# Two mixtures of experts in one network kernel: finished rows out of the first, other memory and PSUM pools at the start of the second

## The chip, the cores and the metric

The kernel runs on one core of a Trainium2 chip. The metric is the device time of one execution in microseconds. Each kernel is run several times, and the median stands for it. A profile of one further execution shows every instruction of the five engines: TensorE (PE, its weight loads PEld), VectorE (DVE), ScalarE (ACT), GpSimd (POOL), and SyncE (SP), which here only issues DMA transfers.

## The reference

The reference is a network of four layers on a graph of 2708 nodes with 256 features in fp32. Each layer adds a graph part and a feed-forward part to `x`, both on a layer norm of `x`:

```python
x = x + gnn(layernorm(x), adj, ...)      # L0 cosine attention, L1 GAT of 4 heads, L2 and L3 GAT of one head
x = x + ffn(layernorm(x), ...)           # L0 slices, L1 first mixture, L2 decoder with second mixture, L3 linear
```

The change touches the two mixtures. The first (layer 1) sends every node to one of eight experts:

```python
H = gelu(xf @ W1 + b1)                                   # 2708 x 1024, common to all experts
probs = softmax(H @ Wg + bg)
assign = argmax(probs)
out = sum over e: where(assign == e, probs[:, e] * (H @ Wd[e] + bd[e]), 0)
```

The second is the feed-forward half of a decoder block (layer 2). Causal attention of four heads comes first, and then every node goes to its two best of eight experts:

```python
x = x + attention(rmsnorm(x, ln1)) @ wo.T
flat = rmsnorm(x, ln2)
tp, ti = top_k(softmax(flat @ router_w.T), 2); tp = tp / sum(tp)
out = sum over e: weights[:, e] * ((silu(flat @ w1[e].T) * (flat @ w3[e].T)) @ w2[e].T)   # HID 682
```

## The kernel before, in words

`X` holds the node features in on-chip memory (SBUF) as 22 row tiles of 128 nodes, the last of 20. All parts of the network read it and add into it. The program is written with tiles and pools: a tile waits for whatever last used its memory, and where a pool is opened over memory of a pool that has been closed, the first writer of each new tile waits for the last user of the old one. Within an engine the order is the scheduler's, and `issue_after` pins an instruction behind another one.

**First mixture** (`top1_ffn`, 980 to 1258 us of the span). Blocks of four row tiles are taken through W1 and gelu. `store` turns the 1024 hidden values of each node back to rows and writes them from SP to `hidden`, a table in DRAM with one row per node. The router's `logits` are made on the way, and `Routing.chunk` places each node in a slot of its expert and scatters the node numbers into `fnodes` from POOL. When all of it has landed, `numbers` reads the list back, and a loop (`through`, 26 slot tiles) goes over tiles of 128 slots which belong to one expert each: `fetch` gathers 128 rows of `hidden` by an indirect DMA into one of five `hr` buffers, `transposes` turns them on TensorE into `ht`, sixteen matmuls with `wd` give `y`, DVE adds the bias into `ys`, and `Routing.send` scatters the rows to `fys`, a table in DRAM in the order of the nodes. `route.weights` computes the chosen probability of every node once (softmax8) while the first rows are fetched. `combine` then loads `fys` into tiles `y0` and sums `X += weight * y` by a DVE instruction per row tile.

**GAT g2** (`gat_single`) starts as soon as the first four tiles of `X` are summed: layer norm statistics, `f`, transposes `tp`, projections `pv`, and then the long loop of `acc` products (L1483). g3, after the second mixture, is the same function. For the second mixture `combine` has another branch: `X` itself lies in the table `dys` from before (`keep` writes it there), the experts' results are added to it by the scatter, and nine SP loads bring finished rows back into `X`.

**Attention and the second mixture** (`attention`, `experts`; 1516 to 2298 us). Attention goes over six column groups of up to 512 nodes. After the last key tile of a group, `close` sums the denominators `pd` on TensorE and DVE divides (`reciprocal`, multiply into `yt`, or `yl` for the last group). `send` of a group then takes it through `wo` (`wy`), adds a normalised X (`xa`), forms the row `h` for the experts, its router logits and the slots, and scatters `h` from POOL into `hs`, the experts' table in DRAM. These sends run spread over the next group's attention. The last group's send runs beside the first expert tiles, and the eight scatters of the last but one group come at the very end of attention. The rows of the first eight slot tiles are loaded into X's tiles (free by then, since the rows are kept in `dys`) ahead of that, and two of them are transposed there.

`experts` takes slot tiles through `h` = w1 (half 0, then SiLU) and w3 (half 1, then the gate), transposes `pt`, and w2 (`po`). The w3 weights (`w<-in_d_w3T`) are loaded by SP at the handover. Its PSUM pools and its SBUF pools `e_work` and `e_r` lie over those of attention: `ss`, `xa`, SiLU's `warm` tile and `hh` are their first tiles. Both halves of `h` lie in one pool `e_h` of four banks, of which one was attention's.

Of the kernel before, what the change touches and what calls it, by code (L numbers as in the profile page):

```python
# [35 lines left out]
def rows(t):  # L36
    return min(P, N - t * P)
# [957 lines left out]
def softmax8(nc, pool, p, n, r, name):  # L995

    m = pool.tile([P, n], F32, name=f"{name}x")
    b = m[:r].unsqueeze(2).to_broadcast([r, n, 8])
    nc.vector.tensor_reduce(m[:r], p, AX.X, ALU.max)
    nc.vector.tensor_tensor(p, p, b, ALU.subtract)  # L1000
    nc.scalar.activation(p, p, AF.Exp)
    nc.vector.tensor_reduce(m[:r], p, AX.X, ALU.add)
    nc.vector.reciprocal(m[:r], m[:r])
    nc.vector.tensor_tensor(p, p, b, ALU.mult)


def top1_ffn(net, ctx):
# [7 lines left out]
    with ExitStack() as inner:  # L1015
# [19 lines left out]
        rows_of = dram.tile([N, HID], F32, name="hidden")  # L1035

        with tc.tile_pool(name="f1tp", bufs=2, space=PSUM) as ptp, tc.tile_pool(
# [57 lines left out]
            def gate(its, halves, nw):  # L1095
                ht = [half[:, k, :] for half in halves for k in range(KC // 2)]
                pq = pg.tile([P, 512], F32, name="pq")
                for c in range(KC):
                    g = c % 4 * 32
                    nc.tensor.matmul(pq[g : g + 32, :nw], wg[:, c, :], ht[c][:, :nw], start=c < 4, stop=c >= 4)  # L1100
                q4 = rp.tile([P, 512], F32, name="q4", tag="hr", bufs=3)
                nc.vector.tensor_copy(q4[:, :nw], pq[:, :nw])
                pr = pg.tile([P, 4, E], F32, name="pr")
                for k, t in enumerate(its):
                    r = rows(t)
                    nc.tensor.matmul(pr[:r, k, :], q4[:, k * P : k * P + r], add4, start=True, stop=True)
                    nc.vector.tensor_tensor(route.logits[:r, t, :], pr[:r, k, :], bg[:r], ALU.add)
                for _ in route.chunk(rp, pg, its[0], len(its), None):
                    pass
# [13 lines left out]
            for n, (n0, nw) in enumerate(blocks):  # L1123
                its = tiles_of(n0, nw)
                halves = hidden(ft, nw)
                if n + 1 < len(blocks):
                    ft = features(tiles_of(*blocks[n + 1]))
                if n == 0:
                    for m in range(3, len(blocks)):
                        turn(add, m, ptp, "tp")  # L1130
                        turn(stats.sums, *tiles[m], root=False)
                    turn(stats.newton, rp, tiles[3][0], NT)
                    last = None
                    held.close()
                    wd = inner.enter_context(tc.tile_pool(name="f1wd", bufs=1, side="right"))
                    wd = wd.tile([P, E, KC, D], F32, name="wd")
                gate(its, halves, nw)
                kept.append((its, halves))
                if n + 2 < len(blocks):

                    stored = store(*kept.pop())
                    with tc.issue_after(stored.ins):
                        for e in range(2 * n, 2 * n + 2):
                            nc.sync.dma_start(wd[:, e], a["f1_wd"][e].rearrange("(c p) m -> p c m", p=P))
# [9 lines left out]
        with tc.tile_pool(name="f1t", bufs=1, space=PSUM) as pt, tc.tile_pool(  # L1154
# [34 lines left out]
            def fetch(s):  # L1189
                hr = held[s] = sp.tile([P, 2, 4, P], F32, name="hr", bufs=5)  # L1190
                return nc.gpsimd.indirect_dma_start(
                    out=hr.rearrange("p n c m -> p (n c m)"),
                    out_offset=None,
                    in_=rows_of[:, :],
                    in_offset=bass.IndirectOffsetOnAxis(ap=number[:, s : s + 1], axis=0),
                )

            def transposes(s):
                hr = held.pop(s)
                ht = sp.tile([P, 2, 4, P], F32, name="ht")  # L1200
                for n in range(2):
                    ps = pt.tile([P, 4, P], F32, name=f"ht{n}", bufs=2)
                    for c in range(KC // 2):
                        nc.tensor.transpose(ps[:, c, :], hr[:, n, c, :], net.ident)
                    (nc.scalar.copy if n else nc.vector.tensor_copy)(ht[:, n], ps)
                return ht

# [19 lines left out]
            route.weights(one)  # L1227
            heads = []

            def through(s0, s1, ready):  # L1230
                last = added = folding = None
                for s in range(s0, s1):
                    with tc.issue_after(last.ins) if last else nullcontext():
                        e = expert(nc.tensor, s)
                    this = ready
                    if s + 1 < s1:
                        ready = transposes(s + 1)
# [8 lines left out]
                    added = nc.vector.tensor_tensor(y, ps, bd[:, e, :].rearrange("p e d -> p (e d)"), ALU.add)  # L1246
# [325 lines left out]
class Routing:  # L1572
# [10 lines left out]
    def __init__(self, net, pool, dram, choices, key):  # L1583
# [12 lines left out]
        self.weight = pool.tile([P, choices, NT], F32, name=f"{key}weight")  # L1596
# [56 lines left out]
    def chunk(self, work, psum, t0, n, source, tag="pr"):  # L1653
# [42 lines left out]
        to = work.tile([P, self.choices, n], I32, name=f"{key}to")  # L1696
# [153 lines left out]
    def weights(self, work):  # L1850

        nc, E = self.net.nc, self.E
        p = work.tile([P, NT, E], F32, name=f"{self.key}p")
        nc.vector.tensor_copy(p, self.logits)
        softmax8(nc, work, p, NT, P, f"{self.key}sm")
        for c in range(self.choices):
            pc = work.tile([P, NT, E], F32, name=f"{self.key}pc")
            nc.vector.tensor_tensor(pc, p, self.one[:, c], ALU.mult)
            nc.vector.tensor_reduce(self.weight[:, c, :], pc, AX.X, ALU.add)

# [48 lines left out]
    def combine(self, pool):  # L1909

        net, nc, X = self.net, self.net.nc, self.net.X
        loaded = []
        queues = nc.sync, nc.gpsimd
        if self.choices == 2:
            for t0, t1 in ((0, 1), (1, 2), (2, 4), (4, 8), (8, 12), (12, 16), (16, 20), (20, NT)):
                for k0, k1, r in whole_and_rest(range(t0, t1)):
                    r0 = (t0 + k0) * P
                    self.read = nc.sync.dma_start(
                        X[:r, t0 + k0 : t0 + k1, :],
                        self.ys[r0 : r0 + (k1 - k0 - 1) * P + r, :].rearrange("(t p) d -> p t d", p=r),  # L1920
                    )
            yield
            return
        for n, (n0, nw) in enumerate(chunks(512)):
            its = tiles_of(n0, nw)
            ys = []
            for c in range(self.choices):
                y = pool.tile([P, 4, D], F32, name=f"y{c}", bufs=len(chunks(512)))
                for k0, k1, r in whole_and_rest(its):
                    r0 = (c * NT + its[k0]) * P  # L1930

                    engine = nc.scalar if n == 0 and c else queues[(n + c) % 2]
                    read = engine.dma_start(
                        y[:r, k0:k1, :],
                        self.ys[r0 : r0 + (k1 - k0 - 1) * P + r, :].rearrange("(t p) d -> p t d", p=r),
                    )
                    if engine is nc.gpsimd:
                        self.read = read
                ys.append(y)
            loaded.append((its, ys))  # L1940
        for its, ys in loaded:
            for k, t in enumerate(its):
                r = rows(t)
                for c, y in enumerate(ys):
                    last = nc.vector.scalar_tensor_tensor(
                        X[:r, t, :], y[:r, k, :], self.weight[:r, c, t : t + 1], X[:r, t, :], ALU.mult, ALU.add
                    )
            yield last


def attention(net, route, ln2, router, weights, mixture):
# [11 lines left out]
    with ExitStack() as ctx:  # L1963
# [98 lines left out]
        outs, sums, es = {}, {}, {}  # L2062
# [48 lines left out]
        def close(n, p):  # L2111
# [8 lines left out]
            for i in range(0, iw, half):  # L2120
                y = results[n][:, p : p + m, i : i + half]
                nc.vector.reciprocal(y, by_pairs(pd, m, iw)[:, :, i : i + half])  # L2122
                nc.vector.tensor_tensor(y, y, by_pairs(po, m, iw)[:, :, i : i + half], ALU.mult)

        def send(n, rp, aux, tag="aux"):
# [4 lines left out]
            nc.vector.memset(ss, 1.0)  # L2130
            xs, hs = {}, {}
            for k, t in enumerate(its):
# [4 lines left out]
                net.normed(xa, t, ln)  # L2137
                nc.vector.tensor_tensor(xa[:r], po[:r], xa[:r], ALU.add)
                nc.gpsimd.tensor_tensor(X[:r, t, :], X[:r, t, :], xa[:r], ALU.add)
                h = hs[t] = rp.tile([P, D + 4], F32, name="h", bufs=len(its) + 1)  # L2140
# [128 lines left out]
def experts(net, route, weights, head, first, fts, after, rest):  # L2269
# [7 lines left out]
    with ExitStack() as ctx:  # L2277
        work = ctx.enter_context(tc.tile_pool(name="e_work", bufs=2))
        pf = ctx.enter_context(tc.tile_pool(name="e_f", bufs=1, space=PSUM))
        ph = ctx.enter_context(tc.tile_pool(name="e_h", bufs=1, space=PSUM))  # L2280
        py = ctx.enter_context(tc.tile_pool(name="e_y", bufs=1, space=PSUM))
# [25 lines left out]
        def hidden(s, n, q):  # L2307
            if q == 0:
                halves[s, n] = ph.tile([P, 2, 512], F32, name=f"h{n}")
# [30 lines left out]
        def results(s, ht):  # L2340
            po = py.tile([P, D], F32, name="po")
            for k in range(KC):
                last = nc.tensor.matmul(  # L2343
                    po, ht[:KP, k, :], w2[:KP, es[s], k, :], start=k == 0, stop=k == KC - 1
# [3 lines left out]
            nc.scalar.activation(y, po, AF.Copy, scale=share)  # L2348
# [98 lines left out]
def biased_gnn(net, head, route):  # L2447
    def results(ctx):
        return route.combine(ctx.enter_context(net.tc.tile_pool(name="g2y", bufs=1)))
# [4 lines left out]
def elu_gnn(net, kept, head, route, tail):  # L2454
    def results(ctx):
        rest = route.combine(ctx.enter_context(net.tc.tile_pool(name="g3y", bufs=1)))
# [219 lines left out]
```

## Time and profile before

| | us |
|---|---|
| median of 3 runs | 2573.68 (2572.01 to 2580.48) |
| profiled execution | 2582.8 |
| its span, first to last instruction | 2580.9 |
| TensorE busy in it | 2420.4 |
| mean granted TensorE clock | 0.967 |

In the lines of the profile that follow, a row of the timeline gives the start, the duration, the engine, the source line, the operation, what it writes and reads, and in brackets the idle time of the engine before it with what ended that. A row of the chain of waits gives a start, a duration and who held the chain. "x8" is the number of instructions that are drawn together.

### The profile page before, as it was taken

To read this page: it belongs to the slowest core of one execution; us is meant where nothing else is said; L and a number is where in the kernel's file an instruction comes from. 1 tells how busy PE (TensorE), PEld (TensorE's weight loads), DVE (VectorE), ACT (ScalarE), POOL (GpSimd) and SP (SyncE) were. 2 spreads that over 40 slices of the span, in tenths; PEclk is the share of its full clock that TensorE was granted. 3 is DMA by queue.
4 is the path that set the end of the run, shared out by engine and by line. 5 is a ranking of instruction groups with operands and counts; after the bars stand their busy time and mean duration, and the time that the engine had idled before them with its cause. 6 is when DMAs were issued, how large, how long until landed. Compare 5 with 4: busy or idle time off the path is not lost.

```text
span 2580.9 us, 32654 instructions
## 1 busy us (share of the span) xinstructions
PE 2420.4 (94%) x11708; PEld 1575.2 (61%) x11708; DVE 1473.2 (57%) x3362; ACT 1049.6 (41%) x1687; POOL 357.0 (14%) x465
## 2 busy tenths in 40 slices
PE   5899998999999999979799989999979999979999
PEld 4666765686333334558678864444457777757887
DVE  7753437745888886433544457878853222243566
ACT  3444443213877782321344333434422222234444
POOL 1000003100000001134230011222222211210011
PEclk9999999969999999989899999999989999989999
DMA  8899512000000002665230010101332222140001
GB/s 287 291 290 345 186 47 73 1 6 1 1 1 1 1 1 84 161 175 168 78 94 1 1 33 17 36 18 50 112 112 49 34 34 34 27 146 29 1 1 44
DMA packets 113657, 197.98 MB, mean 77 GB/s; under 512 B 8898, under 2 KB 72768, under 8 KB 110658
## 3 DMA queue, kind: packets, MB, share of 16 engines
q1 hardware_dynamic: 92008, 150.88, 18.3%
q0 software_dynamic: 18496, 40.89, 6.3%
q10 hardware_dynamic: 2990, 4.06, 0.5%
q8 instruction: 98, 1.61, 0.3%
q14 instruction: 65, 0.53, 0.1%
HBM read 132.97 MB, written 62.83 MB: 76 GB/s over the span
## 4 chain that ended last, share of the span: by engine, by line
PE 42%; DVE 5%; DMA 3%; ACT 1%; issue 1%; POOL 0%; SPq 0%; DVEq 0%; POOLq 0%; ACTq 0%
PE acc L1483 14%; PE h L2311 8%; PE po L2343 4%; PE sc L2078 3%; PE po L2103 3%; PE pv L143 2%; PE pj L2049 2%; DMA dys<-y,to 2%; DVE sum L2109 2%; PE pt L2335 1%; DVE yt L2122 1%; PE acc L143 1%; PE s1p L1378 1%; PE wy L143 1%; DVE e L736 1%
## 5 line engine op out<-in xcount | busy, mean ns | idle before, releaser
L736 DVE SCALAR_TENSOR_TENSOR e<-e,mask 128x768 f32<-128x768 f32 (+3 forms) x352 | 418.1, 1218 | 222.2 <-ACT e L735 218.8
L735 ACT ACTIVATE e<-big_p,minus_one,ratio 128x768 f32<-128x768 f32 (+3 forms) x352 | 418.8, 1226 | 278.2 <-PE acc L1483 189.9
L1483 PE MATMUL acc<-V,e 128*128 128x257 f32 x1848 | 404.3, 381 | 5.7 <-DVE e L736 5.5
L1483 PEld LDWEIGHTS acc<-V,e 128*128 128x128 f32 x1848 | 351.3, 190 | 58.5 <-issue 6.5
L2311 PE MATMUL h<-w,ft 128*128 (+1 forms) x720 | 222.1, 450 | 0.0
L311 PE MATMUL acc<-F,e 128*128 128x257 f32 (+1 forms) x924 | 212.5, 383 | 3.8 <-DVE e L307 3.5
L932 PE MATMUL acc<-e,V 128*64 128x512 f32 (+1 forms) x1056 | 209.6, 549 | 1.3 <-DVE e L736 1.3
L311 PEld LDWEIGHTS acc<-F,e 128*128 128x128 f32 (+1 forms) x924 | 171.6, 189 | 56.6 <-DVE e L307 29.3
L2328 DVE TENSOR_TENSOR hh<-hh,h 128x682 f32<-128x682 f32 x47 | 40.7, 866 | 240.5 <-PE h L2311 240.5
L932 PEld LDWEIGHTS acc<-e,V 128*64 128x64 f32 x1056 | 73.8, 138 | 151.5 <-issue 145.9
L2311 PEld LDWEIGHTS h<-w,ft 128*128 128x128 f32 x720 | 129.1, 189 | 52.2
L307 DVE TENSOR_TENSOR e<-e,mask 128x512 f32<-128x512 f32 (+2 forms) x132 | 80.4, 620 | 140.8 <-ACT e L300 139.1
L2087 ACT ACTIVATE e<-sc 128x1024 f32<-128x1024 f32 (+4 forms) x131 | 107.2, 862 | 113.5 <-PE sc L2078 89.1
L2109 DVE TENSOR_TENSOR sum<-sum,e 128x1024 f32<-128x1024 f32 (+4 forms) x131 | 136.7, 1043 | 20.3 <-PE po L2103 11.2
L300 ACT ACTIVATE e<-score 128x512 f32<-128x512 f32 (+2 forms) x132 | 69.4, 544 | 170.7 <-PE score L298 145.3
L2343 PE MATMUL po<-w,ht 114*128 (+1 forms) x564 | 129.7, 379 | 0.9 <-DVE ht L2336 0.9
L2078 PE MATMUL sc<-qt,kt 64*128 64x512 f32 (+5 forms) x568 | 120.5, 542 | 1.4 <-ACT sum L2087 0.9
L2343 PEld LDWEIGHTS po<-w,ht 114*128 114x128 f32 x564 | 106.5, 189 | 22.6 <-DVE ht L2336 8.2
L943 PE MATMUL den<-e,low 128*3 128x512 f32 (+1 forms) x1056 | 117.7, 542 | 0.0
L298 PE MATMUL score<-QK 128*128 128x512 f32 (+2 forms) x264 | 112.1, 553 | 3.4 <-ACT e L300 3.0
L2103 PE MATMUL po<-e,V 128*64 128x512 f32 (+5 forms) x524 | 106.9, 525 | 1.9 <-DVE e L2093 1.9
L1895 POOL DMA_INDIRECT dys<-y,to x47 | 73.6, 1567 | 202.6 <-ACT ft L2293 184.5
(652 smaller groups left out, 3378.0 us busy)
## 6 DMA issues: line engine op xcount, KB each, us to landing
row<-in_adj SPq DMA_DIRECT2D x21, 1354.0 KB
raw<-in_adjT SPq DMA_DIRECT2D x35, 768.0 KB
hs<-zero SPq DMA_DIRECT2D x8, 2860.0 KB
hidden<-hr SPq DMA_DIRECT2D x32, 256.0 KB
wd<-in_f_wd SPq DMA_DIRECT2D x8, 1024.0 KB
kept<-mask SPq DMA_DIRECT2D x21, 338.5 KB
mask<-kept SPq DMA_DIRECT2D x21, 338.5 KB
w<-in_d_w1T SPq DMA_DIRECT2D x8, 682.0 KB
```

Source lines behind the costliest of these rows:

```text
L298: nc.tensor.matmul(ps[:r, :iw], QK[:, 0, span(j)], QK[:, 1, i0 : i0 + iw], start=True, stop=True)
L311: ended = nc.tensor.matmul(acc[k], e[:r, k * P : (k + 1) * P], F[:r, j, :], start=j == 0, stop=j == NT - 1)
L735: nc.scalar.activation(v, big_p[:, i], AF.Relu, bias=net.minus_one, scale=ratio)
L736: return nc.vector.scalar_tensor_tensor(v, v, 1.0, net.mask[:, j, i], ALU.add, ALU.mult)
L932: nc.tensor.matmul(acc[n][half, :iw], V[:, j, h, :], e[n][:, k, :iw], start=j == 0, stop=j == NT - 1)
L943: nc.tensor.matmul(den[g : g + Q, :iw], low[:, j, h, Q - 1 - q : 2 * Q - 1 - q], e[n][:, k, :iw], start=False, stop=j == NT - 1 and q == Q ...
L1483: nc.tensor.matmul(acc[k][:ri], e[:, k * P : k * P + ri], V[:, j, :], start=j == 0, stop=j == NT - 1)
L2078: nc.tensor.matmul(by_pairs(ps[:r, g], m, iw)[:, :, o:], kt[b, span(j)], qt[b, :, o:iw], start=True, stop=True)
L2103: nc.tensor.matmul(by_pairs(outs[n, p][b], m, iw)[:, :, o:], V[:r, j, g, :], by_pairs(e[:r, g], m, iw)[:, :, o:], start=j == 0, stop=j == ...
L2109: nc.vector.tensor_tensor(total, total, by_heads(e[:r], m, iw)[:, :, :, o:], ALU.add)
L2311: last = nc.tensor.matmul(halves[s, n][:, q, :HALF], fts[s][:, c, :], weights.w13[n][:, es[s], c, q * HALF : (q + 1) * HALF], start=c == 0 ...
L2343: last = nc.tensor.matmul(po, ht[:KP, k, :], w2[:KP, es[s], k, :], start=k == 0, stop=k == KC - 1)
```

## The change

In the first mixture the rows of `hidden` become longer: 1024 hidden values, the node's eight logits and its 256 values of `X`. `keep_rows` writes the two additions from POOL. The fetched row then holds all that is needed for the finished result: `share` computes the probability of the chosen expert from the logits per slot tile (maximum, subtraction, exp with a sum on ACT, reciprocal), and one more DVE instruction forms `ys * share + X`. `softmax8`, `Routing.weights` and the first branch of `combine` go. `fys` now holds finished rows, and both mixtures load them into `X` by the same nine SP transfers. `ht` has two buffers rather than three.

In the second mixture, the `h` rows of the last but one send are put into tiles of `X` that are free then (from tile 11 on) rather than into the pools which the experts take over. The slots `to` get two buffers in the routing's own pool. The experts' PSUM is opened as separate pools, in the order `e_f`, `e_h0` (half 0), `e_y` (`po`), `e_h1` (half 1) and `e_t` (`pt`), so that half 0 no longer shares a bank with attention's `po`. And in `send`, the memset of `ss` and the normalised `xa` are pinned behind the multiply that ended the last `close`.

```diff
-        rows_of = dram.tile([N, HID], F32, name="hidden")
+        rows_of = dram.tile([N, HID + E + D], F32, name="hidden")
+
+        def keep_rows(its, at, src):
+            for k0, k1, r in whole_and_rest(its):
+                r0 = its[k0] * P
+                nc.gpsimd.dma_start(
+                    rows_of[r0 : r0 + (k1 - k0 - 1) * P + r, at : at + src.shape[2]].rearrange("(t p) d -> p t d", p=r),
+                    src[:r, its[k0] : its[k0] + k1 - k0, :],
+                )
...
+                keep_rows(its, HID, route.logits)
...
                 kept.append((its, halves))
+                keep_rows(its, HID + E, X)
...
-                hr = held[s] = sp.tile([P, 2, 4, P], F32, name="hr", bufs=5)
+                hr = held[s] = sp.tile([P, HID + E + D], F32, name="hr", bufs=5)
...
-                hr = held.pop(s)
-                ht = sp.tile([P, 2, 4, P], F32, name="ht")
+                hr = held[s][:, :HID].rearrange("p (n c m) -> p n c m", n=2, c=4)
+                ht = sp.tile([P, 2, 4, P], F32, name="ht", bufs=2)
...
+            def share(s):
+
+                logits = held[s][:, HID : HID + E]
+                top, w = (sp.tile([P, 1], F32, name=n) for n in ("top", "share"))
+                nc.vector.tensor_reduce(top, logits, AX.X, ALU.max)
+                nc.vector.tensor_scalar(logits, logits, top, None, ALU.subtract)
+                nc.scalar.activation(logits, logits, AF.Exp, accum_out=w)
+                nc.vector.reciprocal(w, w)
+                return w
...
-            route.weights(one)
...
+                    with tc.issue_after(added.ins) if added else nullcontext():
+                        w = share(s)
                     if s + 1 < s1:
                         ready = transposes(s + 1)
...
-                    added = nc.vector.tensor_tensor(y, ps, bd[:, e, :].rearrange("p e d -> p (e d)"), ALU.add)
+                    nc.vector.tensor_tensor(y, ps, bd[:, e, :].rearrange("p e d -> p (e d)"), ALU.add)
+                    added = nc.vector.scalar_tensor_tensor(y, y, w, held.pop(s)[:, HID + E :], ALU.mult, ALU.add)
...
-        to = work.tile([P, self.choices, n], I32, name=f"{key}to")
+        to = self.pool.tile([P, self.choices, 4], I32, name=f"{key}to", bufs=2)[:, :, :n]
...
+    def combine(self):
+
+        for t0, t1 in ((0, 1), (1, 2), (2, 4), (4, 8), (8, 12), (12, 16), (16, 20), (20, NT)):
+            for k0, k1, r in whole_and_rest(range(t0, t1)):
+                r0 = (t0 + k0) * P
+                self.read = self.net.nc.sync.dma_start(
+                    self.net.X[:r, t0 + k0 : t0 + k1, :],
+                    self.ys[r0 : r0 + (k1 - k0 - 1) * P + r, :].rearrange("(t p) d -> p t d", p=r),
+                )
+        yield
...
-                nc.vector.tensor_tensor(y, y, by_pairs(po, m, iw)[:, :, i : i + half], ALU.mult)
+                ended[:] = [nc.vector.tensor_tensor(y, y, by_pairs(po, m, iw)[:, :, i : i + half], ALU.mult)]
...
-            nc.vector.memset(ss, 1.0)
+            with tc.issue_after(ended[0].ins):
+                nc.vector.memset(ss, 1.0)
...
-                net.normed(xa, t, ln)
+                with tc.issue_after(ended[0].ins):
+                    net.normed(xa, t, ln)
...
-                h = hs[t] = rp.tile([P, D + 4], F32, name="h", bufs=len(its) + 1)
+                if n + 2 == len(cols):
+                    h = done[:, 11 * D + k * (D + 4) : 11 * D + (k + 1) * (D + 4)]
+                else:
+                    h = rp.tile([P, D + 4], F32, name="h", bufs=len(its) + 1)
+                hs[t] = h
...
-        ph = ctx.enter_context(tc.tile_pool(name="e_h", bufs=1, space=PSUM))
-        py = ctx.enter_context(tc.tile_pool(name="e_y", bufs=1, space=PSUM))
+        ph = [ctx.enter_context(tc.tile_pool(name="e_h0", bufs=1, space=PSUM))]
+        po = ctx.enter_context(tc.tile_pool(name="e_y", bufs=1, space=PSUM))
+        ph.append(ctx.enter_context(tc.tile_pool(name="e_h1", bufs=1, space=PSUM)))
+        py = ctx.enter_context(tc.tile_pool(name="e_t", bufs=1, space=PSUM))
```

More of the change, by code (lines that the diff above doesn't have):

```diff
@@ L992, in first_max @@
     return oh, mx
[L995 to L1004, printed above, removed]
 def top1_ffn(net, ctx):
@@ L1189, in fetch @@
             def fetch(s):
-                hr = held[s] = sp.tile([P, 2, 4, P], F32, name="hr", bufs=5)
+                hr = held[s] = sp.tile([P, HID + E + D], F32, name="hr", bufs=5)
                 return nc.gpsimd.indirect_dma_start(
-                    out=hr.rearrange("p n c m -> p (n c m)"),
+                    out=hr,
                     out_offset=None,
@@ L1595, in __init__ @@
         self.one = pool.tile([P, choices, NT, E], F32, name=f"{key}one")
-        self.weight = pool.tile([P, choices, NT], F32, name=f"{key}weight")
         self.tag = pool.tile([P, NT, 4], F32, name=f"{key}tag")
@@ L1848, in others @@
             yield
[L1850 to L1859, printed above, removed]
     def load(self, s, f):
@@ L1907, in send @@
         return i
[L1909 to L1948, printed above, removed]
+    def combine(self):
[7 more added lines that the diff above has]
+        yield
 def attention(net, route, ln2, router, weights, mixture):
@@ L2060, in by_heads @@
             return t[..., : m * iw].rearrange("p g (m i) -> p g m i", m=m)
-        outs, sums, es = {}, {}, {}
+        outs, sums, es, ended = {}, {}, {}, []
         def scores(n, p, j):
@@ L2308, in hidden @@
             if q == 0:
-                halves[s, n] = ph.tile([P, 2, 512], F32, name=f"h{n}")
+                halves[s, n] = ph[n].tile([P, 2, 512], F32, name=f"h{n}")
             for c in range(2):
@@ L2340, in results @@
         def results(s, ht):
-            po = py.tile([P, D], F32, name="po")
+            ps = po.tile([P, D], F32, name="po")
             for k in range(KC):
                 last = nc.tensor.matmul(
-                    po, ht[:KP, k, :], w2[:KP, es[s], k, :], start=k == 0, stop=k == KC - 1
+                    ps, ht[:KP, k, :], w2[:KP, es[s], k, :], start=k == 0, stop=k == KC - 1
                 )
@@ L2347, in results @@
             to, share = tos.pop(s)
-            nc.scalar.activation(y, po, AF.Copy, scale=share)
+            nc.scalar.activation(y, ps, AF.Copy, scale=share)
             route.send(to, y)
@@ L2448, in results @@
     def results(ctx):
-        return route.combine(ctx.enter_context(net.tc.tile_pool(name="g2y", bufs=1)))
+        return route.combine()
     gat_single(net, "g2", head, results)
@@ L2455, in results @@
     def results(ctx):
-        rest = route.combine(ctx.enter_context(net.tc.tile_pool(name="g3y", bufs=1)))
+        rest = route.combine()
         first = next(rest)
```

## The prediction

> **What bounds the kernel now.** I read the page's busy table first, then the chain of waits, then the timeline at the chain's steps that are not TensorE, and last the DMA view there.
>
> ```profile
> PE 2420.4 (94%) x11708; PEld 1575.2 (61%) x11708; DVE 1473.2 (57%) x3362; ACT 1049.6 (41%) x1687; POOL 357.0 (14%) x465
> ...
> 1258.80 6.63 DMA y<-fys
> 1269.60 3.53 PE pv L143 x8
> ...
> 1889.68 5.90 DMA hs<-h,dto
> 1896.46 1.92 DVE yl L2122
> 1898.93 4.92 PE h L2311 x8
> ```
>
> TensorE is busy 94% of the span, and the change removes next to no matmul. So only TensorE's idle time, 160 us in all, can be won. The chain shows two idle places that the diff touches: the end of the first mixture (from 1257.8) and the handover from attention to the second mixture (from 1886). The timeline has both:
>
> ```profile
> 1255.36 0.96 POOL L1895 DMA_INDIRECT fys<-ys,to  x1 [2.49 <-DVEq L1847]
> 1257.92 1.51 SPq L1933 DMA_DIRECT2D y<-fys  x3
> 1261.75 1.67 DVE L1945 SCALAR_TENSOR_TENSOR X<-y,fweight,X 128x256 f32<-128x256 f32 x4 [3.07 <-DMA y<-fys]
> 1269.53 3.59 PE L143 MATMUL pv<-g2w,ft 128*128 128x257 f32 x8
> ...
> 1885.46 0.72 PE L2117 MATMUL pd<-sum,ones 128*64 128x296 f32 x4 [0.29 <-ACT X L2255]
> 1886.27 6.79 SPq L1568 DMA_DIRECT2D w<-in_d_w3T  x8
> 1889.68 0.96 POOL L1707 DMA_INDIRECT hs<-h,dto  x1 [0.30 <-issue]
> 1895.73 0.06 DVE L2130 MEMSET ss<- 128x4 f32 x1 [11.09 <-DMA hs<-h,dto]
> 1896.39 1.99 DVE L2122 RECIPROCAL yl<-pd 128x296 f32<-128x296 f32 x1
> 1898.93 4.92 PE L2311 MATMUL h<-w,X 128*128 128x341 f32 x8 [12.75 <-DVE yl L2123]
> 1903.64 1.33 PE L143 MATMUL wy<-wo,yl 128*128 128x256 f32 x4
> 1904.81 2.46 PE L2311 MATMUL h<-w,X 128*128 128x341 f32 x8
> ```
>
> At the handover DVE stands at the memset of ss until the last scatter of hs has landed, and the reciprocal queued behind it needs only pd, finished at 1886.18. TensorE's first expert product (h, half 0) waits 12.75 us for that DVE chain, since its PSUM tile shares a bank with attention's po. It then runs at half clock: 4.92 us for eight, against 2.46 us for the eight of half 1. From there on TensorE is full until 2291.
>
> **The change, part by part.** *1. Handover.* The h rows of the last but one send move out of the pools which the experts take over, the slots `to` too, and half 0 has its own banks. In the changed order DVE runs reciprocal and multiply of yl before ss and xa, and h half 0 waits for no DVE instruction. Step by step from 1886.18: h half 0 at 1886.3 to 1888.8 (2.46 us, the clock being full until then); yl done at 1886.3 + 1.99 + 0.1 + 0.46 = 1888.9; wy 1.04 us to 1890. Next is h half 1, which needs the first w3 expert. Its eight DMAs of 682 KB are issued from 1886.27 as before, beside the scatters. What moved, in the table by stretches (start:end, length, busy times, clock, DMA share, GB/s):
>
> ```profile
> 1886.00:1888.00 2.00, 0.18 (x2) 0.00 (x0) 0.00 (x0) 0.00 (x0) 1.70 (x2) 1.00 0.58 102
> 1888.00:1890.00 2.00, 0.00 (x0) 0.00 (x0) 0.00 (x0) 0.00 (x0) 1.39 (x3) 1.00 0.88 295
> 1890.00:1892.00 2.00, 0.00 (x0) 0.00 (x0) 0.00 (x0) 0.00 (x0) 0.65 (x1) 0.65 1.01 338
> ```
>
> By 1891 that is 0.20 + 0.59 + 0.34 = 1.13 MB, of which up to 0.5 MB are scatters; 0.68 MB of w3 fit. If the queue serves its transfers in order, expert 0 has landed at 1890.8 to 1891.5, and half 1 starts at 1891.4 instead of 1904.81: **-13.4 us**. The Trainium skill speaks against the order ("DMA: Bandwidth & Descriptors", section "Queues, rings and completion order"): completion is not FIFO per issuing engine, and an engine takes packets from its queues in turn. With all eight transfers sharing alike, expert 0 would end near 1904 and only -0.5 us would be left. The nearest row decides: of nine loads issued together on SP at 2297.98 the first (128 KB) let DVE start 1.97 us later, far ahead of the rest.
>
> ```profile
> 2297.98 5.22 SPq L1918 DMA_DIRECT2D X<-dys  x9
> 2299.95 0.43 DVE L164 BATCH_NORM_STATS2 bnst<-X 128x6 f32<-128x256 f32 x1 [6.45 <-DMA X<-dys]
> ```
>
> I take -13.3; ends -0.5 and -14. The eight scatters stay POOL's; the hh memset ahead of them waits for the same cast that they wait for. SiLU's table load (1.28 us) goes ahead of ACT's copies of X: ACT idles 2.24 us there, so 0; without that gap, +1.3. Later weights come every 1.7 us (682 KB at 400 GB/s), where a tile takes 8.16 us, and the first eight tiles' rows were loaded at 1794 to 1798.
>
> *2. End of the first mixture.* Rows come out finished, so the y tiles and 22 DVE sums go (0.42 to 0.48 us each, 10 us); nine SP loads write X itself, starting with one tile. From fys landed (1257.77) to the first loop product (1312.22) are 54.45 us. GAT g3 has just that form after the second mixture: landed 2297.91, loop 2347.24, 49.33 us. **-5.1**; -8 if all the sums lay on the path, -4 if they hide more. The w2 loads, which waited for the y tiles, start up to 28 us earlier, behind X's loads on SP: 0.
>
> *3. First mixture's loop.* A tile takes TensorE 4.33 us (26 tiles). DVE had 0.42 + 0.69; the share adds a reduce, subtract, reciprocal (0.17 each), a wait for ACT's exp (0.4) and the final sum (0.48). In sequence with gaps some 3.3 to 3.9 us, under 4.33: **0**; the last tile's sum lies bare: **+0.5**. A fetched row grows from 4096 to 5152 bytes, and its buffer (five) is freed by the sum rather than by the transposes:
>
> ```profile
> L1191 POOL DMA_INDIRECT hr<-hidden,number x26: 933/962/1021, 1134.7 to 1227.2; - x26
> ...
> DMA to landing us min/median/max: 4.1/4.8/8.5
> ```
>
> After sum s come the send (1.28 us of POOL with its gap), then fetch s+5, whose rows are wanted when y of s+3 ends, 3 x 4.33 - 1.0 us after sum s: a lead of about 10 us. 1.26 times the bytes make 4.8 us 6.0: 0. The first fetches, which nothing covers (5.07 us idle for the first, 0.45 for the second), get longer: **+0.7**. The removed weights (2.3 us of DVE, exp) lay beside this wait: 0.
>
> *4. Its preparation.* X (seven DMAs, 2.77 MB) and the logits (seven, 2708 pieces of 32 bytes) go out on POOL's queue ahead of and between the fnodes scatters, each of which they delay by at most two issues (1.3 us each). X is final by 1018.4; only 0.15 of the DMA time is used in 1000 to 1020 and the first scatters wait until 1024.78, so at 255 GB/s about 9 of 11 us of writes fit before the rest disturbs; TensorE's lead covers most. In 1115 to 1130 the DMA is full and bounds the first fetch. There the page's section "Specifications" warns: below 512 B a transfer misses line rate, by a read-modify-write. The fnodes pieces (4 bytes) are the row: 192 of them took 1.3% of 16 engines over 17 us, 0.018 us each. The last two groups of logits, 660 pieces, are then 660 x 0.018 / 16 = 0.75 us of the full stage; priced double for the rule, 1.5. I take **+1** for the stage (0 to +3.5; +14.6 if all of X, at 190 GB/s, displaced the stores).
>
> *5. Attention.* DVE is 9.67 of 12 us busy before the first projection (TensorE idles 6.08 us at 1516.44 to 1522.52). ss and two pairs of xa leave there: 0.49 + 0.53 + 0.40 + 0.40 + 0.06 = **-1.9**. They come back behind a multiply later, where TensorE has 19 to 20 of 20 us busy and DVE slack: 0 (-1 to +2).
>
> Sum: -13.3 - 5.1 + 0.5 + 0.7 + 1 - 1.9 = **-18**. The profiled execution took 2582.8 us (span 2580.9) and would become 2565; the median of the runs is 2573.7, 9 us less, so I subtract from that: **2556 us**.
>
> **The rivals.** *(a) The w3 weights become the bound.* The wait moves from yl to the first w3 expert at 1904. For it: 5.6 MB at 400 GB/s end just then. Against: the row of nine loads. Sum: -18 + 12.8 = -5, 2568. *(b) Slower: the fetch lead.* At the loop of the first mixture each fetch depends on the sum five tiles back. The cycle spans four tiles, so beyond a landing of L = 10 us every tile costs (L - 10)/4, over 26 tiles 6.5 us per us of L. L = 12.8 eats the gain, L = 14 makes +8 us, 2582. For it: a landing of 8.5 us occurs already, times 1.26 is 10.7. Against: the median is 4.8 and the DMA is 0.45 busy in 1150 to 1250. *(c) DVE or ACT turns becomes the loop's pace:* the share's hops through ACT take 0.4 us a tile more than TensorE's 4.33: +10, so -8, 2566. *(d) The change does nothing:* pools or queues still hold the wait in another form (a bank, a queued memset), -5 to 0, 2571.
>
> **How the numbers follow.** About 0.3%, 7.7 us, is what a measurement of this kernel tells from no change. The forecast has 0.68 (own range 2548 to 2565), (a) 0.10, (b) 0.09, (c) 0.08, (d) 0.05. Faster by over 7.7 us: 0.66 of the forecast, half of (c), a little of (a): 0.72. Slower: (b) and a full collision of X's writes together with (a): 0.10. Within: 0.18. The range 2547 to 2571 takes in (a), (c) and most of (d).
>
> **What would show it.** After: DVE's recip yl straight after pd, before ss; h half 0 starts within 1 us of pd, at 2.46 us for eight; half 1 waits 1 to 2 us for w3 (12 us: rival a). From fys landed to g2's loop 49 to 50 us. The loop at 4.33 us a tile, PE waiting for hr only at its start (each later wait: rival b; for ht: c). From the first hidden store to the first transposes at most 2 us longer. The forecast is wrong if h half 0 still names DVE, or if the front keeps its 54 us.

## The result, and the profile after

The changed kernel takes 2563.63 us (median of 16 runs, 2557.04 to 2572.08), the kernel before 2580.36 us in the same series (16 runs). The ratio of the two is 0.9943, with a 95% interval of 0.9930 to 0.9956. That is a gain of 14.7 us, between 11.4 and 18.1 (the medians lie 16.7 us apart, the means 14.7). The prediction said 2556 us, 18 us less than the three runs then known. Their median was 2573.68 us, and that of all sixteen is 6.7 us more, so most of the 7.6 us between 2556 and 2563.63 comes from the base and not from the change.

The page of the changed kernel shows TensorE still at 94% of a shorter span:

```profile
span 2562.0 us, 32785 instructions
...
PE 2418.0 (94%) x11708; PEld 1572.4 (61%) x11708; DVE 1485.3 (58%) x3436; ACT 1057.3 (41%) x1738; POOL 364.2 (14%) x475
```

The timeline of the changed kernel at the end of the first mixture:

```profile
1254.09 0.96 POOL L1893 DMA_INDIRECT fys<-ys,to  x1 [2.49 <-DVE ys L1256]
1256.58 5.79 SPq L1912 DMA_DIRECT2D X<-fys  x9
...
1258.54 0.43 DVE L164 BATCH_NORM_STATS2 bnst<-X 128x6 f32<-128x256 f32 x1 [0.93 <-DMA X<-fys]
...
1264.57 3.78 PE L143 MATMUL pv<-g2w,ft 128*128 128x257 f32 x8
```

The layer norm starts 1.96 us after the first load was issued, where the first sum of `X` had come 3.83 us after it. The first projection follows 7.99 us after the load instead of 11.61. The handover to the second mixture, in the same view:

```profile
1880.84 0.72 PE L2085 MATMUL pd<-sum,ones 128*64 128x296 f32 x4 [0.24 <-ACT X L2229]
...
1881.49 2.56 PE L2287 MATMUL h<-w,X 128*128 128x341 f32 x8
1881.61 2.01 DVE L2090 RECIPROCAL yl<-pd 128x296 f32<-128x296 f32 x1 [1.19 <-PE pd L2085]
1881.65 7.23 SPq L1578 DMA_DIRECT2D w<-in_d_w3T  x8
...
1884.07 0.06 DVE L2099 MEMSET ss<- 128x4 f32 x1
...
1884.17 1.13 PE L143 MATMUL wy<-wo,yl 128*128 128x256 f32 x4
...
1886.01 0.96 POOL L1716 DMA_INDIRECT hs<-X,dto  x1 [0.30 <-issue]
...
1886.25 2.53 PE L2287 MATMUL h<-w,X 128*128 128x341 f32 x8 [0.95 <-DMA w<-in_d_w3T]
```

Half 0 of `h` follows `pd` at once and at full clock (2.56 us for eight), `yl` stands ahead of `ss`, and `ss` is written before the last scatter has even been issued. Half 1 starts 4.6 us after the first w3 load was issued and waits only 0.95 us for it.

The whole program by stages, in us from event to event, one profile each (two of before, of the changed kernel and of the decoder's part alone):

| stage | before | changed | decoder only | rows only | pin_ends |
|---|---|---|---|---|---|
| start to first fetch of hr | 1134.7, 1135.4 | 1131.7, 1135.3 | 1132.7, 1133.0 | 1130.9 | 1137.8 |
| first transposes to second tile's ys | 11.8, 11.9 | 12.8, 13.1 | 12.6, 12.0 | 11.5 | 11.5 |
| second to last ys of the loop | 103.6, 103.6 | 103.6, 103.6 | 103.6, 103.6 | 103.6 | 103.6 |
| last ys to first load of results | 3.3, 3.2 | 3.7, 3.7 | 3.5, 3.5 | 3.7 | 3.7 |
| first load to g2's loop | 54.3, 54.4 | 49.4, 49.1 | 54.7, 54.5 | 48.7 | 48.8 |
| g2's loop | 204.2, 204.2 | 205.8, 205.9 | 205.9, 205.9 | 205.7 | 205.6 |
| end of the loop to attention's first tp | 6.1, 6.1 | 4.8, 4.8 | 4.8, 4.8 | 6.2 | 4.8 |
| first tp to end of pd | 363.7, 363.7 | 365.0, 370.3 | 366.1, 366.0 | 363.6 | 362.6 |
| end of pd to h half 1 | 18.6, 18.7 | 4.7, 4.9 | 4.5, 5.2 | 18.6 | 4.7 |
| h half 1 to the first load of X from dys | 393.2, 392.0 | 392.1, 391.9 | 392.2, 392.2 | 392.0 | 392.8 |

The transposes in the second row are `ht`, and `tp` are those of attention, which the prediction and the expectations call its first projection. What comes after the last row (g3 and the linear layer, untouched) took 283.7 and 280.0 us in the two profiles of the changed kernel, and the stages before the first fetch differ as much. Two rows carry the gain, the front of g2 and the handover. Two rows speak against it: g2's loop and attention.

### The profile page after: what moved, and what is told of

Its sections match the earlier page's. It is cut to its first block, busy times and chain, and to the rows that moved or that the text cites. A ratio compares the mean times of both kernels' runs of the same rounds, so it can differ in the third digit from the quotient of the medians.

```text
span 2562.0 us, 32785 instructions
## 1 busy us (share of the span) xinstructions
PE 2418.0 (94%) x11708; PEld 1572.4 (61%) x11708; DVE 1485.3 (58%) x3436; ACT 1057.3 (41%) x1738; POOL 364.2 (14%) x475
## 4 chain that ended last, share of the span: by engine, by line
PE 82%; DVE 9%; DMA 4%; ACT 2%; issue 1%; POOL 0%; SPq 0%; DVEq 0%; ACTq 0%; POOLq 0%
PE acc L1493 15%; PE acc L932 8%; PE h L2287 8%; PE acc L311 7%; PE den L943 5%; PE po L2319 4%; PE score L298 4%; PE y L1249 3%; PE sc L2046 3%; PE po L2071 3%; PE pv L143 3%; PE h L1069 2%; PE pj L2017 2%; DMA dys<-y,to 2%; DVE sum L2077 2%; PE po L143 1%
## 5 line engine op out<-in xcount | busy, mean ns | idle before, releaser
L2077 DVE TENSOR_TENSOR sum<-sum,e 128x1024 f32<-128x1024 f32 (+4 forms) x131 | 137.3, 1048 | 20.8 <-PE po L2071 11.4
```

The costliest lines, as they stand in the source:

```text
L2077: nc.vector.tensor_tensor(total, total, by_heads(e[:r], m, iw)[:, :, :, o:], ALU.add)
```

## The experiments

`decoder`, `rows` and `pin_ends` were timed against the kernel before. The others were executed once: `one_bank_pool` 2559.62 us, `h_in_pool` 2562.37, `no_pin` 2564.39, `hr4` 2568.54, `x_twice` 2573.32, `to_in_pool` 2573.87. Single executions of the changed kernel lie 15 us apart, so of these runs only the stages are read.

**The two parts alone.** `decoder` keeps only the edits to the routing's slots, `attention` and `experts`, `rows` only those to the first mixture and to `combine`:

```diff
 # decoder: the first mixture and combine as before, for instance
-        rows_of = dram.tile([N, HID + E + D], F32, name="hidden")
+        rows_of = dram.tile([N, HID], F32, name="hidden")
 # rows: the decoder as before, for instance
-        ph = [ctx.enter_context(tc.tile_pool(name="e_h0", bufs=1, space=PSUM))]
+        ph = ctx.enter_context(tc.tile_pool(name="e_h", bufs=1, space=PSUM))
```

> Only the second mixture's part (h rows in X, slots in their own pool, PSUM pools, ss and xa pinned), the first mixture as before. Theory that the parts add up: the handover from the end of pd to the first w3 product falls from 18.6 us to about 4.7 us (-13.9), the start of attention gains 1.3 us, the first mixture keeps its 54.3 us from the first load of results to g2's loop: -15 us in all. Rival, that the decoder's gain is partly paid back in attention (the profile after shows 1.4 us more from the first projection to pd): -13 us or less, with that stage longer than 363.5 us here too.

Measured: 2567.04 us against 2577.73, ratio 0.9955 (0.9940 to 0.9971), -11.6 us. The handover gives 14.1 and 13.4 us here in two profiles, and the start of attention 1.3. Attention is 2.4 us longer than before in both profiles, so the rival's clause is met.

> Only the first mixture's part (longer rows, share, finished rows loaded into X), the decoder as before. Theory: -4.9 us from the first load of results to g2's loop, +0.8 from the first hidden store to the first fetch, +1.1 at the first two fetched tiles, +0.5 at the last tile: -2.5 us, handover still 18.6 us. Rival, that the longer rows pay the front's gain back (larger fetches, X written beside the stores): 0 to +5 us, to be seen as a loop over 4.33 us a tile or a stage from store to fetch over 126 us.

Measured: 2576.59 us, ratio 0.9992 (0.9980 to 1.0004), -2.1 us with an interval that holds no change. The front of g2 is 5.6 us shorter, the loop keeps 4.33 us a tile, the handover stays at 18.6. The parts add up: -11.6 and -2.1 make -13.7, and both together gave -14.7; the intervals are wide enough for that.

**What made the wait at the handover.** Three edits lie there, and three kernels take one of them back. The first takes back the PSUM pools:

```diff
-        ph = [ctx.enter_context(tc.tile_pool(name="e_h0", bufs=1, space=PSUM))]
-        po = ctx.enter_context(tc.tile_pool(name="e_y", bufs=1, space=PSUM))
-        ph.append(ctx.enter_context(tc.tile_pool(name="e_h1", bufs=1, space=PSUM)))
-        py = ctx.enter_context(tc.tile_pool(name="e_t", bufs=1, space=PSUM))
+        ph = [ctx.enter_context(tc.tile_pool(name="e_h", bufs=1, space=PSUM))] * 2
+        po = py = ctx.enter_context(tc.tile_pool(name="e_y", bufs=1, space=PSUM))
```

> The changed kernel with both halves of h in one PSUM pool and po with pt, as before. Theory, that the bank passes on only the wait for yl, and that yl is early by itself now: h half 0 starts 2.5 us after pd instead of at once, h half 1 some 6.2 us after pd instead of 4.7: +1.5 us. Rival, that the shared bank made the wait (the profile before names yl as the releaser of 12.75 us): the handover goes back to 17 us or more, +12 us.

```profile
1882.48 2.56 PE L2285 MATMUL h<-w,X 128*128 128x341 f32 x8 [2.60 <-DVE yl L2091]
...
1885.74 2.46 PE L2285 MATMUL h<-w,X 128*128 128x341 f32 x8
```

Measured: half 0 waits 2.60 us for `yl`, half 1 comes 5.86 us after `pd` instead of 4.69: with the memory moves in place, the bank is worth 1.2 us. The "12.75 <-DVE yl" of before was the last link of a chain, not its cause.

The second puts the rows back into the pool:

```diff
-                if n + 2 == len(cols):
-                    h = done[:, 11 * D + k * (D + 4) : 11 * D + (k + 1) * (D + 4)]
-                else:
-                    h = rp.tile([P, D + 4], F32, name="h", bufs=len(its) + 1)
+                h = rp.tile([P, D + 4], F32, name="h", bufs=len(its) + 1)
```

> The changed kernel with the h rows of the last but one send back in the pool that the experts take over. Theory: yl is computed ahead of ss, so h half 0 and half 1 of the first tile start as in the changed kernel (half 1 4.7 us after pd), but SiLU's first tiles wait for the scatters to land, and h half 0 of the second tile, which needs half 0's bank back, comes 6 to 8 us later: +6 to +8 us. Rival, that these rows alone made the wait of before: half 1 of the first tile is late by 12 us and all of the handover's gain is gone.

The timeline of h_in_pool:

```profile
1882.50 0.17 DVE L1685 COPY dso_far<-dcount 128x8 f32<-128x8 f32 x1 [11.13 <-DMA hs<-h,dto]
1882.58 2.00 DVE L2090 RECIPROCAL yl<-pd 128x296 f32<-128x296 f32 x1
...
1885.13 2.08 PE L143 MATMUL wy<-wo,yl 128*128 128x256 f32 x4 [9.72 <-DVE yl L2091]
1886.99 4.38 PE L2284 MATMUL h<-w,X 128*128 128x341 f32 x8
```

Half 0 ran at once, thanks to its banks, but half 1 came 14.1 us after `pd` (+9.4 us). My theory missed that: I had looked for `ss` ahead of `yl` and not for the copy to `dso_far`. It is another first tile in the recycled memory. DVE had it ahead of `yl` here (behind `yl` in the kernel before), and it waits for the scatters just the same. `wy` stands between half 0 and half 1 on TensorE and passes the wait on. TensorE then runs more slowly (4.38 us for the eight of half 1, 2.53 in the changed kernel).

The third takes back the pool of the slots:

```diff
-        to = self.pool.tile([P, self.choices, 4], I32, name=f"{key}to", bufs=2)[:, :, :n]
+        to = work.tile([P, self.choices, n], I32, name=f"{key}to")
```

> The changed kernel with the slots in the pool of the send again, as before. Theory, by the row of h_in_pool (14.1 us from pd to h half 1, since a DVE instruction ahead of yl took memory that the scatters read): the slots are read by the same eight scatters and lie in the same pools, so the handover goes to 12 to 14 us, +7 to +9. Rival, that the scatter's index list is free once the instruction has been issued: the handover stays below 7 us.

```profile
1883.27 0.96 POOL L1716 DMA_INDIRECT hs<-X,dto  x1 [0.31 <-issue]
...
1889.25 0.17 DVE L1685 COPY dso_far<-dcount 128x8 f32<-128x8 f32 x1 [11.94 <-DMA hs<-X,dto]
1889.33 2.00 DVE L2090 RECIPROCAL yl<-pd 128x296 f32<-128x296 f32 x1
...
1893.75 4.58 PE L2287 MATMUL h<-w,X 128*128 128x341 f32 x8
```

Measured: 14.9 us from `pd` to half 1, +10.2. The `h` rows were out of the pool here, yet the slots, 32 bytes a partition, hold DVE until the last scatter has landed, 5 us after POOL had issued it. So either of the two moves is worth little without the other: of the 13.9 us, 4.5 and 3.7 are left.

**The pins in attention.** `no_pin` removes them all, `pin_ends` keeps them in the first and the last send:

```diff
-            with tc.issue_after(ended[0].ins):
-                nc.vector.memset(ss, 1.0)
+            pin = n in (0, len(cols) - 1)
+            with tc.issue_after(ended[0].ins) if pin else nullcontext():
+                nc.vector.memset(ss, 1.0)
...
-                with tc.issue_after(ended[0].ins):
-                    net.normed(xa, t, ln)
+                with tc.issue_after(ended[0].ins) if pin else nullcontext():
+                    net.normed(xa, t, ln)
```

> The changed kernel without the pins on ss and xa in send. Theory, that the pins move DVE work from the start of attention into its middle and give it back there: the idle before the first projection returns from 4.8 to 6.1 us, the stage from the first projection to pd falls from 365.0 to 363.6 us, the handover stays at 4.7 us since ss no longer waits for the scatters: 0 in sum. Rival, that the pins are what brings yl ahead of ss: the handover goes back by 10 us or more.

Measured (one profile): 6.1 us before the first transposes, 363.6 us to `pd`, 5.5 us at the handover: the theory's numbers, but for 0.8 us at the handover, where half 1 waited 1.73 us for w3. The pins in sum win nothing, and they are not what frees the handover.

> The changed kernel with ss and xa pinned only in the first send (the one that fell into the start of attention) and the last (at the handover), the sends between as before. Theory, that the pins of the middle sends are what lengthens attention: the idle before the first projection stays at 4.8 us, the stage from the first projection to pd falls to 363.6 us, the handover stays at 4.7 us: -1.4 us against the changed kernel, about 2562. Rival, that the first send's pin alone sets the order of attention: the stage keeps 365 us or more and nothing is won.

Measured: 2558.49 us against 2576.28, ratio 0.9926 (0.9912 to 0.9940). In its profile the start keeps 4.8 us, attention falls to 362.6 and the handover stays at 4.7. It is the best of the kernels that were timed more than once, but its interval overlaps that of the changed kernel (0.9930 to 0.9956), so a further gain is not shown by the times. By the profiles the middle pins do lengthen attention: from `tp` to `pd` it took 365.0 to 370.3 us in all nine profiles that have them, and 362.6 to 363.7 us in all five that don't. Two waits are longer with them. In the timelines of before, of the changed kernel and of pin_ends, in this order:

```profile
1662.95 1.98 PE L2049 MATMUL pj<-ft,wq 128*128 128x512 f32 x4 [0.85 <-DVE xa L2138]
...
1876.74 0.41 PE L1686 MATMUL rank<-dtaken,dbefore 128*128 128x32 f32 x2 [1.04 <-DVE dtaken L1674]
```

```profile
1656.51 2.41 PE L2017 MATMUL pj<-ft,wq 128*128 128x512 f32 x5 [1.57 <-DVE xa L2108]
...
1872.17 0.41 PE L1695 MATMUL rank<-dtaken,dbefore 128*128 128x32 f32 x2 [1.56 <-DVE dtaken L1683]
```

```profile
1659.81 2.84 PE L2017 MATMUL pj<-ft,wq 128*128 128x512 f32 x6 [0.86 <-DVE xa L2109]
...
1873.61 0.41 PE L1695 MATMUL rank<-dtaken,dbefore 128*128 128x32 f32 x2 [1.04 <-DVE dtaken L1683]
```

With the middle pins TensorE waits 0.72 us longer for an `xa` and 0.52 us longer for `dtaken`, which DVE computes late. Another wait of 0.74 us goes, so TensorE idles only 0.6 us more in this stage than in pin_ends. The rest of the 2.4 us between the two profiles is the clock: it fell in the changed kernel after a wait of 1.81 us in the middle of the stage, and stayed full in pin_ends after the same wait. In other profiles it fell behind `dtaken` instead. The stretch of 5 us in which the rank products lie, in before and in the decoder's part alone (columns as in the prediction's table by stretches: start:end, length, busy times of PE, PEld, DVE, ACT and POOL, clock, DMA share, GB/s):

```profile
1877.00:1882.00 5.00, 4.78 (x36) 2.39 (x35) 4.46 (x21) 1.22 (x2) 1.60 (x2) 1.00 0.07 26
```

```profile
1877.00:1882.00 5.00, 4.69 (x24) 2.55 (x26) 4.12 (x24) 1.23 (x2) 1.07 (x3) 0.74 0.00 0
```

A clock of 0.74 over 5 us is worth some 1.3 us of TensorE time, by an estimate from that row (0.26 of 5 us). A drop there was seen in four of the nine profiles with the middle pins, and in none of the five without. The other five of the nine have the drop behind that wait of 1.8 us, and so has one of the five without the pins, the second of the kernel before. Whether the pins bring the drop, and how, is not shown.

**The fetch lead.** One buffer fewer tries the cycle of rival (b):

```diff
-                hr = held[s] = sp.tile([P, HID + E + D], F32, name="hr", bufs=5)
+                hr = held[s] = sp.tile([P, HID + E + D], F32, name="hr", bufs=4)
```

> The changed kernel with four hr buffers rather than five. By the prediction's cycle, one tile less of lead: three tiles of 4.33 us (13.0) against 7.7 us of fixed steps plus a landing of 4.7 us (12.4): the loop just keeps 4.33 us a tile, 0. Rival, that the lead was shorter than reckoned: 0.3 us or more on every tile, +8 us or more in the loop, with TensorE waiting for hr.

The loop took 4.7 us more, all of it at one tile (9.0 us); the others kept 4.33. Neither side had that. The timeline of hr4 shows it on POOL's queue:

```profile
1160.93 0.98 POOL L1893 DMA_INDIRECT fys<-ys,to  x1 [2.95 <-DVE top L1210]
1161.91 0.77 POOL L1290 DMA_DIRECT2D g2w<-in_g_w  x1
1162.67 0.61 POOL L106 DMA_DIRECT2D av<-in_g_a  x1
1163.23 0.59 POOL L1296 DMA_DIRECT2D g2bv<-in_g_b  x1
1164.12 1.02 POOL L1189 DMA_INDIRECT hr<-hidden,number  x1 [0.30 <-issue]
...
1170.57 1.93 PE L1202 MATMUL ht<-ident,hr 128*128 128x128 f32 x8 [2.81 <-DMA hr<-hidden,number]
```

Three loads for g2 (640 KB) come between a send and the next fetch. They delay its issue by 2 us and share the DMA with it, and with four buffers there is no slack for that. Of the 4.7 us, 2.81 are the wait in the last row; from 1170 to 1175 us the clock was 0.66, which is some 1.7 us more by an estimate (0.34 of 5 us). With five buffers there is. The changed kernel has the same three loads in the same place (`--tile hr` gives the time from issue to landing):

```profile
DMA to landing us min/median/max: 4.5/4.7/9.4
```

Its rows are 26% longer than before, and its loop kept 103.6 us.

**The writes of X.** Each was sent twice:

```diff
-                keep_rows(its, HID + E, X)
+                for _ in range(2):
+                    keep_rows(its, HID + E, X)
```

> The changed kernel with each write of X into the rows of hidden sent twice, another 2.77 MB on POOL's queue. Theory, that these writes lie in idle DMA time ahead of the stores: the first fetch at most 2 us later than in the other profiles (1124 to 1135 us of the span). Rival, that they displace the stores at 190 to 255 GB/s: 11 to 14 us later, after 1140 us.

The first fetch came at 1135.3 us of the span, inside the spread of the other profiles (1124.3 to 1137.8). From the first store into `hidden` to that fetch it took 122.0 us, and 117.5 to 123.7 in the others. TensorE stays busy while the DMA is full, in the table by stretches of x_twice:

```profile
1020.00:1040.00 20.00, 19.44 (x88) 9.79 (x86) 9.81 (x48) 6.25 (x10) 7.08 (x10) 1.00 0.99 264
```

In the changed kernel the DMA's share of the same stretch was 0.78, so the edit did load it. The 2.77 MB more cost nothing that can be seen, and the collision of the slower rival's kind did not come. In the changed kernel three of the seven writes go out before 990 us, long before the stores. The long whole time of x_twice comes later: attention took 370.0 us and g2's loop 207.3, both in part at a clock near half. A cost of one or two us can't be told from this spread.

**Second profiles.**

> The kernel before once more, for a second profile. Theory, that its first profile was lucky in the g2 loop (204.2 us, full clock from the first product, where every other profile has 205.6 or more with a start at 0.7 of the clock): 205.6 us or more here. Rival, that the changed front itself brings the slower start: 204.2 us again. The stages before the change's first store and fetch are expected to differ from the first profile by some us in either case.

> The decoder's part alone once more, for a second profile. Open is the g2 loop: 204.2 us with full clock from its first product in both profiles of the kernel before, 205.6 us or more in every kernel with the change, and 205.9 us also here, where g2's front is that of before. Theory, that the clock at the loop's first 5 us is a matter of chance from run to run: 204.2 us this time, or anything else than 205.9. Rival, that something in the decoder's part sets it: 205.9 us again with a clock near 0.66.

> The changed kernel once more, for a second profile: 4.7 us from pd to h half 1, 48.5 to 49.5 us from the first load of X to g2's loop, g2 loop 205.6 us or more if the changed front sets its clock, the stage from the first projection to pd at 365 us or more if the middle pins set that.

The g2 loop of before took 204.2 us again, so its first profile was no luck; my theory fell. The decoder's part alone took 205.9 us again, with g2's front of before. The part `rows`, with the decoder of before, took 205.7. So chance alone is unlikely to set it, and either part of the change brings the slower loop. The first 5 us of the loop tell the difference, in before and then in the decoder's part alone:

```profile
1312.20:1317.20 5.00, 4.97 (x23) 4.41 (x24) 2.66 (x4) 1.03 (x1) 0.00 (x0) 1.00 0.45 143
```

```profile
1311.40:1316.40 5.00, 5.00 (x16) 4.08 (x17) 1.56 (x2) 0.89 (x1) 0.00 (x0) 0.66 0.45 143
```

TensorE waits 2.77 us ahead of the loop in both. In one the clock stays full, in the other it falls to about half within the first 2.5 us. What in the change decides that stays open. The second profile of the changed kernel has the handover and the front as expected, and 370.3 us of attention: there DVE and ACT stood for 3.3 and 4.7 us just before `pd`, with nothing that the profile can name ("remote"), and TensorE waited 4.27 us before `pd`. The cause of that stays open too.

## Why the prediction was right or wrong

The direction, the place and the mechanism held; the 18 us were 3 us too many against the measured 14.7, within the interval of 11.4 to 18.1. That the sum came so near is partly luck: 1.7 us charged for the preparation and the first fetches do not show, and offset half of the 3 us by which attention and g2's loop got longer.

*Handover.* Predicted -13.3 us, measured -13.9 (18.6 to 4.7). The first w3 load was needed 4.5 to 5.2 us after its issue by the estimate, and half 1 started 4.6 us after it. Following the row of nine loads was right: of eight transfers of 682 KB issued together, the first was usable at 4.6 us, not when all 5.6 MB were through. The rule of the Trainium skill which I set against it ("DMA: Bandwidth & Descriptors", section "Queues, rings and completion order") does not say the contrary: it is about completions that can overtake one another, and the same section has each engine consume its descriptors "in ring order". That eight transfers of one issuer share alike was my reading, and the runs refute it. Rival (a) is out. Where I wrote that half 0 waits for DVE because it shares a bank, the bank was worth only 1.2 us once the memory moves were in; the two moves carry it together.

*End of the first mixture.* Predicted -5.1 us by comparing with g3; 4.9 and 5.3 us in two profiles of the changed kernel, 5.6 in the part alone.

*Loop.* Predicted 0; the loop is 103.6 us with and without the longer rows. Rivals (b) and (c) are out. The bare last sum costs 0.4 us, as reckoned. "First fetches +0.7" was too much: from the first fetch's issue to the first transposes it went from 4.59 to 4.69 us; the first two tiles show 11.5 to 13.1 us with the longer rows and 11.8 to 12.6 without.

*Preparation.* Predicted +1 us. From the first store to the first fetch it took 123.0 and 119.2 us before and 123.7 and 120.3 in the changed kernel; with 3.8 us between two profiles of one kernel, +1 is neither shown nor excluded. x_twice shows nothing beyond the spread.

*Attention.* This is the term that was mis-sized. "-1.9" at its start was -1.3: four `xa` and the memset left DVE, but TensorE's wait shrank from 6.08 to 4.77 us only. And "they come back ... 0" was +1.4 us (1.36 before rounding) in the changed kernel's first profile and +2.4 in the part alone, where the prediction allowed -1 to +2: the middle pins make `xa` and `dtaken` late, and the clock fell behind a wait in each of these profiles. In pin_ends and no_pin the stage is as short as before.

*Not in the sum:* g2's loop, +1.6 us, by the clock in its first 5 us.

With these terms the sum by stages is -13.9 - 4.9 + 0.4 - 1.3 + 1.4 + 1.6 = -16.7 us for the first profile of the changed kernel; the first profiles of the two kernels lie 18.9 us apart in span, and the measured gain is 14.7.

## What to carry to other kernels

The wait that a profile names can be only the last link of a chain: take back one edit at a time to see which one carries it. Where memory is recycled, every reader of it has to go, down to a list of slots, and every instruction ahead of the wanted one on its engine has to be looked at. Work that is pinned out of one busy place comes back in another, so pin only the instance that stands in the way.

## What the runs showed of the hardware that was not expected

TensorE's clock fell after waits that are short. After one of 1.81 us in the changed kernel's attention, the next stretch ran at 0.66:

```profile
1725.00:1730.00 5.00, 5.00 (x16) 1.57 (x16) 5.00 (x9) 0.96 (x5) 2.39 (x2) 0.66 0.00 0
```

The same wait, 1.81 to 1.85 us long, stands in all fourteen profiles. The clock fell behind it in six of them and stayed full in eight; of the two profiles of the kernel before, it fell in the second only. The 2.77 us ahead of g2's loop left the clock full in both profiles of before, and the first 5 us of the loop ran at 0.50 to 0.72 in all twelve profiles of the other kernels. At 0.50 (no_pin and x_twice) the loop took 207.2 and 207.3 us, 3 us more than before. So a short wait of TensorE can be followed by a loss of up to 3 us beyond its own length here, and its length does not tell whether it is. That the wait sets the fall off is read from the order in time alone.
